# Two graph layers and two mixtures of experts on one core: a count matrix sent out in two pieces, the edge stage ahead of routing's constants, and four buffers for attention's first block

## The chip, the cores and the metric

The kernel runs on one core of one Trainium2 chip. A core has TensorE (matrix products into PSUM), VectorE, ScalarE, GpSimd (POOL here) and SyncE (SP, which only issues transfers). Each engine works through its own list of instructions in order and waits on semaphores for the others; SP, ScalarE (ACT) and POOL each issue DMA transfers on a queue of their own, and 16 DMA engines carry them. The metric is the device time of one execution in microseconds. A kernel is run several times, and the median counts.

## The reference, cut to what matters

`x` is 3125 nodes of 256 features, `src` and `dst` are 50,000 edges, `dst` sorted. Four layers, each added to `x` after a layer norm:

```python
edge_index = jnp.stack([src, dst])
x = x + gnn0(layernorm(x), src, dst)       # three graph convolutions, 256 -> 256, degree norms
x = x + ffn0(layernorm(x))                 # 16 experts, top 2 of them, then a layer norm with gamma, beta
x = x + gnn1(layernorm(x), edge_index)     # attention over the edges: 4 heads of 64
x = x + ffn1(layernorm(x))                 # 8 experts, top 2 of the softmax
# gnn0, one convolution:
h = h * norm_src[:, None] @ W
agg = segment_sum(h[src], dst)
out = agg * norm_dst[:, None] + b
# gnn1:
xa = h @ W;  el = xa @ Wl.T;  er = xa @ Wr.T
e = exp(leaky_relu(el[src] + er[dst], 0.2))
w = e / segment_sum(e, src)[src]
heads = [segment_sum(w[:, k:k+1] * xa[dst], src) for k in range(4)]
out = elu(stack(heads) + b)
```

## The kernel before, in words

The nodes are padded to NT = 25 tiles of 128 rows, of which REAL = 125 are nodes and three are padding. The seven destination blocks (BLK) hold 512 nodes four times (four tiles each) and then 384 three times (three tiles each). Both graph layers work with dense matrices of edge counts (how many edges lead from node a to node b), one per block, in fp16. They are built once, kept in DRAM in two layouts (`cnt`, source by destination, and `cntT`, its transpose) and loaded again, in groups of five source tiles, by every graph convolution and by attention.

A planner (Tile) lays out the order of each engine's instructions before the kernel runs. It goes through the program with durations that it assumes; whatever is ready on an engine may be taken, and among ready instructions the one that stands earlier in the program goes first. So a place in the program is a rank, not a time. It also gives out the memory: a tile that takes over another's room waits for the last reader of that room, transfers included.

The stages that matter here, in order:

**Constants.** Lines 707 to 743 make ramps, masks and token numbers for routing; `Router.__init__` (from line 745) makes further ones for each of the two mixtures and loads their gate weights over SP. In the program all of it stands ahead of the edges.

**Edge stage** (lines 1193 to 1311). `src` comes over SP and `dst` over ACT, three transfers each (L1214 to L1218). VectorE turns them into float (`nf`, L1221), then into tile numbers (`til`, L1225, L1226) and pairs (`edge`, L1227, L1228), which are written to DRAM in four shifted copies (`eds`, L1241, two on SP, two on ACT). POOL fills X's last rows with zeros (L1244) and SP loads X (L1246). VectorE finds where in the sorted list each of SG x 128 places begins by 16 comparisons summed up (L1279, L1285), for the first 128 places and then for the other four groups; POOL gathers the edges of each group from `eds` (L1302), and TensorE turns them (L1310) into `by`.

**Counting** (lines 1334 to 1385). For each run of nodes VectorE writes two one-hot matrices (`os`, L1349; `od`, L1352), TensorE multiplies them into counts (`pc`, L1354), ScalarE copies those into `cr` (L1357), which holds a block for all 25 source tiles and has two buffers. POOL clears the padding of `cr` first (L1340). After each destination tile TensorE transposes its columns (L1363), they go to `ct` (two buffers), and seven transfers on SP write them to `cntT` (L1372). After the last tile of a block one transfer on SP writes the whole of `cr` to `cnt` (L1378). At the ninth tile the layer norm's moments of X are taken.

**Graph convolutions** (lines 1407 to 1478). `cnt` is loaded (`cload`, L1421), cast by ScalarE (`ar`, L1452); the features, in two parts (`hi`, L1443, and the rest, L1446, on VectorE; `parts`, L1445, on ScalarE), are multiplied by it on TensorE (L1457). Layer 0 normalises X first (L1440, VectorE).

**End of the first mixture** (lines 1523 to 1594). Per block: two results of experts are added up (`rsum`, L1176), layer norms, `h` (L1554, ScalarE), transposes, the product with W (`px`, L1561, copied to `xT`, L1562), and a small product `py` (L1566), of which ScalarE copies out `xn` (L1567) and the factors `lr` (L1568). `tops` (L1569, VectorE) takes their largest. `xn` lies in the tile `spare`.

**Attention** (lines 1600 to 1746). ScalarE makes `xp`, the four heads' scaled copies of `xn`, tile by tile (L1718). For block b and source tile t VectorE writes the weights of all edges, `e`, four operations (L1730), into one of five buffers (three in HB, one of their own, and last `spare`), and TensorE multiplies them by `xp` (`att`) and sums them (`sums`), both L1618, in a fixed order. The buffer's number is

```python
ring.append(spare)
e = ring[(b * NT + t) % len(ring)]
```

In block b + 1 `finish` completes block b bit by bit, with VectorE and ScalarE work between the tiles. The second mixture follows.

Of the kernel before, what the change touches and what calls it, by code (L numbers as in the profile page):

```python
# [19 lines left out]
P = 128  # L20
# [574 lines left out]
def fast(  # L595
# [56 lines left out]
    consts = ctx.enter_context(tc.tile_pool(name="consts", bufs=1))  # L652
# [5 lines left out]
    cnt = [dram.tile([P, NT, w], F16, name=f"cnt{s0}") for s0, w in BLK]  # L658
    cntT = [dram.tile([P, NT, w], F16, name=f"cntT{s0}") for s0, w in BLK]

    ident = consts.tile([P, P], F32, name="ident")
# [42 lines left out]
                                    op0=OP.subtract, op1=OP.mult)  # L704


    iota_i = consts.tile([P, P], I32, name="iota_i")
    nc.gpsimd.iota(iota_i, pattern=[[1, P]], base=0, channel_multiplier=0)
    iota_r = consts.tile([P, P], F32, name="iota_r")
    nc.vector.tensor_copy(iota_r, iota_i)  # L710
    part_i = consts.tile([P, 1], I32, name="part_i")
    nc.gpsimd.iota(part_i, pattern=[[1, 1]], base=0, channel_multiplier=1)
    part = consts.tile([P, 1], F32, name="part")
    nc.vector.tensor_copy(part, part_i)
    before = consts.tile([P, P], BF16, name="before")
    nc.vector.tensor_scalar(before, iota_r, part, None, op0=OP.is_gt)
    ones = consts.tile([P, P], BF16, name="ones")
    nc.vector.memset(ones, 1.0)
    ones_f = consts.tile([P, P], F32, name="ones_f")
    nc.vector.memset(ones_f, 1.0)  # L720
    part_b = consts.tile([P, P], F32, name="part_b")
    nc.vector.tensor_copy(part_b, part.to_broadcast([P, P]))
    real = consts.tile([P, 1], F32, name="real")
    nc.vector.tensor_scalar(real, part, float(REAL), None, op0=OP.is_lt)
    unreal = consts.tile([P, 1], F32, name="unreal")
    nc.vector.tensor_scalar(unreal, part, float(REAL), None, op0=OP.is_ge)
    PADS = P - REAL
    drop = consts.tile([P, NT], F32, name="drop")
    nc.vector.tensor_scalar(drop, iota_r[:, :NT], float(2 * PADS), None, op0=OP.mult)
    nc.vector.scalar_tensor_tensor(drop, part.to_broadcast([P, NT]), float(-REAL), drop, op0=OP.add, op1=OP.add)  # L730
    assert 2 * NT * PADS <= 2 * P
    tok2 = consts.tile([P, NT], F32, name="tok2")
    nc.vector.tensor_scalar(tok2, iota_r[:, :NT], 2.0 * P, None, op0=OP.mult)
    nc.vector.scalar_tensor_tensor(tok2, part.to_broadcast([P, NT]), 2.0, tok2, op0=OP.mult, op1=OP.add)
    tok_i = consts.tile([P, NT], I32, name="tok_i")
    nc.gpsimd.iota(tok_i, pattern=[[P, NT]], base=0, channel_multiplier=1)


    metas = consts.tile([P, NT, 8], F32, name="metas")
    nc.vector.memset(metas, 0.0)  # L740
    nc.vector.tensor_copy(metas[:, :, 0], tok2)
    nc.vector.tensor_copy(metas.bitcast(I32)[:, :, 5], tok_i)
    places = consts.tile([P, 2, NT], I32, name="places")

    class Router:

# [431 lines left out]


    MAGIC = 12582912.0  # L1180
    ident16 = consts.tile([P, P], F16, name="ident16")
    nc.vector.tensor_copy(ident16, ident)
    ones16 = consts.tile([P, 32], F16, name="ones16")
    nc.vector.memset(ones16, 1.0)
    full = consts.tile([1, 1], F32, name="full")

    state = ctx.enter_context(tc.tile_pool(name="state", bufs=1))
    X = state.tile([P, NT, D], F32, name="X")
    HB = state.tile([P, NT * D], F32, name="HB")
    HBn = HB.rearrange("p (t d) -> p t d", d=D)  # L1190

    R0 = Router("m0", f0_gate_w, f0_gate_b, f0_gate_w.shape[1], False, consts)
    R1 = Router("m1", f1_gate_w, f1_gate_b, f1_gate_w.shape[1], True, consts)
    plans = ctx.enter_context(tc.tile_pool(name="plans", bufs=1))

    with tc.tile_pool(name="edges", bufs=1) as ed, tc.tile_pool(name="ework", bufs=2) as ew:
        by = [ed.tile([P, SG * P], dt, name=f"by{i}") for i, dt in enumerate((F16, F32))]
        with tc.tile_pool(name="epre", bufs=1) as ep, tc.tile_pool(name="ps_pre0", bufs=1, space=PSUM) as ps0, \
# [36 lines left out]
            for k in range(P // ST):  # L1235
# [8 lines left out]
            nc.gpsimd.memset(X[96:], 0.0)  # L1244
            for a, b in ((0, SPLIT), (SPLIT, REAL)):
                nc.sync.dma_start(X[a:b], x.rearrange("(t p) d -> p t d", p=REAL)[a:b])  # L1246


            base = ep.tile([P, SG * P], F32, name="base")
# [22 lines left out]
            for g0, g1 in ((0, 1), (1, SG)):  # L1272
                a, b = g0 * P, g1 * P
                n = 0
                for h in range(CH):
                    for o in range(0, P, ST):
                        one = nf[:, 1, h, o:o + 1]
                        if n == 0:
                            i = nc.vector.tensor_scalar(acc[:, a:b], base[:CR, a:b], one, None, op0=OP.is_gt)  # L1279
# [19 lines left out]
                at_e = ep.tile([P, SG], I32, name=f"at_e{g0}")  # L1299
                sent = nc.vector.tensor_tensor(at_e[:, G], f[:, G, 0], f[:, G, 1], op=OP.add)  # L1300
                for g in range(g0, g1):
                    nc.gpsimd.indirect_dma_start(  # L1302
                        out=got[:, g].rearrange("p e v -> p (e v)"), out_offset=None, in_=rows_e,
                        in_offset=bass.IndirectOffsetOnAxis(ap=at_e[:, g:g + 1], axis=0))
            for g in range(SG):

                nc.scalar.activation(key[:, g, :], got[:, g, :, 1], AF.Identity, bias=f[:, g, 3:4])
                for i, v in enumerate((got[:, g, :, 0], key[:, g, :])):
                    pt = ps_by.tile([P, P], F32, name="pt")
                    nc.tensor.transpose(pt, v, ident)  # L1310
                    nc.scalar.copy(by[i][:, g * P:(g + 1) * P], pt)

        ramp_i = ed.tile([P, 512], I32, name="ramp_i")
        nc.gpsimd.iota(ramp_i, pattern=[[1, 512]], base=0, channel_multiplier=0)
        ramp = ed.tile([P, 512], F16, name="ramp")
# [15 lines left out]
        with tc.tile_pool(name="ps_cnt0", bufs=2, space=PSUM) as ps_cnt0, \  # L1331
# [6 lines left out]
            for b, (s0, bw) in enumerate(BLK):  # L1338
                cr = ew.tile([P, NT, bw], F16, name="cr", tag="cr")
                nc.gpsimd.memset(cr.rearrange("p t (u q) -> p t u q", q=P)[:, :, :, REAL:], 0.0)  # L1340
                for dt in range(s0 // P, (s0 + bw) // P):
                    o = dt * P - s0
# [26 lines left out]
                    for b2, (q0, w2) in enumerate(BLK):  # L1369
                        nc.tensor.matmul(op[b2 // 4][32 * (b2 % 4):32 * (b2 % 4) + 32, :w2], ones16,  # L1370
                                         ct[:, q0:q0 + w2], start=(dt == 0), stop=(dt == NT - 1))
                        nc.sync.dma_start(cntT[b2][:, dt, :], ct[:, q0:q0 + w2])  # L1372
                    if dt == 1:
                        R0.clear(HB[:, 9 * R1.Q:])
                        R1.clear(HB[:, :9 * R1.Q])
                    if dt == 8:
                        mv, r = moments(X)
                nc.sync.dma_start(cnt[b], cr)  # L1378
# [128 lines left out]
    with tc.tile_pool(name="moe0", bufs=1) as mp:  # L1507
# [16 lines left out]
        with tc.tile_pool(name="ps_pre", bufs=2, space=PSUM) as ps, tc.tile_pool(name="tail", bufs=1) as mp:  # L1524
# [12 lines left out]
            for s0, w in BLK:  # L1537
# [26 lines left out]
                py = ps.tile([P, 4, OD + 2 * NH], F32, name="py", tag="py")  # L1564
                for i in range(n):
                    nc.tensor.matmul(py[:, i, :], xT[:, (t0 + i) * P:(t0 + i + 1) * P], turn, start=True, stop=True)  # L1566
                nc.scalar.copy(xn[:, t0:t0 + n, :], py[:, :n, :OD])  # L1567
                nc.scalar.copy(lr.rearrange("p t s h -> p t (s h)")[:, t0:t0 + n, :], py[:, :n, OD:])  # L1568
# [31 lines left out]
    with tc.tile_pool(name="gat", bufs=2) as gp, tc.tile_pool(name="aloads", bufs=2) as loads:  # L1600
        xp = gp.tile([P, NT, NH, OD], F32, name="xp", bufs=1)
        with tc.tile_pool(name="ps_att", bufs=2, space=PSUM) as ps_att, \
# [116 lines left out]
            for b, (s0, w) in enumerate(BLK):  # L1719
# [4 lines left out]
                for kg in range(0, NT, KG):  # L1724
                    a = load_cnt(loads, cntT[b], kg, w)
                    for k in range(KG):
                        t = kg + k
                        e = ring[(b * NT + t) % len(ring)]
                        for h in range(NH):
                            nc.vector.scalar_tensor_tensor(e[:, h, :w], ub[:, h, :w], wj[:, t, h:h + 1],  # L1730
                                                           a[:, k, :w], op0=OP.max, op1=OP.mult)
# [70 lines left out]
```

## Time and profile before

| | us |
|---|---|
| median of 3 runs (2017.44 to 2019.27) | 2019.27 |
| the profiled execution | 2025.07 |
| its span, first to last instruction | 2023.2 |
| TensorE busy | 1850.2 |
| VectorE busy | 1197.2 |
| ScalarE busy | 781.7 |
| edge stage and constants, until the first count | 52.3 |
| counting, until TensorE's last product | 297.2 |
| first graph convolution's first product | 304.9 |
| attention's first product | 1185.2 |
| mean granted TensorE clock, share of full | 0.955 |

Busy is the time in which an engine has an instruction under way; matrix products are pipelined, so a busy TensorE need not be at its peak. The span is also shown in 40 slices of 50.6 us, in each of which a digit gives the busy share in tenths. The timeline lists instructions by start, with like ones merged; in square brackets stands how long the engine was idle before and what ended that. `SPq`, `ACTq` and `POOLq` are the sequencers that issue transfers. The time of an issue is the time until the queue has taken it, not until it has landed. The trace also keeps a record of each packet of a transfer, with its size and time.

### The profile page before, as it was taken

To read this page: it belongs to the slowest core of one execution; us is meant where nothing else is said; L and a number is where in the kernel's file an instruction comes from. 1 tells how busy PE (TensorE), PEld (TensorE's weight loads), DVE (VectorE), ACT (ScalarE), POOL (GpSimd) and SP (SyncE) were. 2 spreads that over 40 slices of the span, in tenths; PEclk is the share of its full clock that TensorE was granted. 3 is DMA by queue.
4 is the path that set the end of the run, shared out by engine and by line. 5 is a ranking of instruction groups with operands and counts; after the bars stand their busy time and mean duration, and the time that the engine had idled before them with its cause. 6 is when DMAs were issued, how large, how long until landed. Compare 5 with 4: busy or idle time off the path is not lost. (4 is left out here: it accounts for less than half of the span.)

```text
span 2023.2 us, 31498 instructions
## 1 busy us (share of the span) xinstructions
PE 1850.2 (91%) x10742; PEld 1220.2 (60%) x10742; DVE 1197.2 (59%) x3811; ACT 781.7 (39%) x1571; POOL 368.8 (18%) x414
## 2 busy tenths in 40 slices
PE   1898979999999999699999979999999998699995
PEld 1444547898899889588898622223223233589893
DVE  7998864113103545544433958988998998444323
ACT  0367776556556555222232660212212222233230
POOL 5000000000000133354551000000300402444430
PEclk9999999999999999699998969999999999599996
DMA  6145664344434444765664401111111111456646
GB/s 165 39 179 213 229 231 132 112 123 134 130 108 143 126 113 125 228 196 189 205 208 145 161 13 53 44 46 51 41 44 50 39 40 29 119 190 201 202 144 198
DMA packets 172296, 259.87 MB, mean 128 GB/s; under 512 B 33476, under 2 KB 116658, under 8 KB 171100
## 3 DMA queue, kind: packets, MB, share of 16 engines
q1 hardware_dynamic: 148446, 211.87, 34.1%
q0 software_dynamic: 16016, 37.00, 5.5%
q10 hardware_dynamic: 7662, 8.84, 1.4%
q8 instruction: 91, 1.49, 0.3%
q14 instruction: 81, 0.66, 0.1%
HBM read 187.38 MB, written 70.27 MB: 127 GB/s over the span
## 5 line engine op out<-in xcount | busy, mean ns | idle before, releaser
L1457 PE MATMUL agg<-ar,parts 128*128 128x512 f32 (+1 forms) x2100 | 446.6, 371 | 7.6 <-ACT parts L1445 7.6
L1457 PEld LDWEIGHTS agg<-ar,parts 128*128 128x128 f32 x2100 | 382.3, 189 | 54.9 <-ACT parts L1445 7.7
L1730 DVE SCALAR_TENSOR_TENSOR HB<-ub,wj,cload 128x512 f32<-128x512 f32 (+1 forms) x420 | 268.5, 687 | 21.7 <-ACT ub L1634 9.9
L1452 ACT CAST ar<-cload 128x2560 fp32r<-128x2560 f16 (+1 forms) x105 | 220.8, 2103 | 145.8 <-PE agg L1457 131.2
L1049 ACT ACTIVATE hid<-ph,b1s 128x128 f32<-128x128 f32 x448 | 128.1, 369 | 315.3 <-PE ph L1045 315.3
L1045 PEld LDWEIGHTS ph<-xsT,w1t 128*128 128x128 f32 x1792 | 222.5, 197 | 25.9 <-DVE xsT L1035 14.6
L1045 PE MATMUL ph<-xsT,w1t 128*128 128x128 f32 x1792 | 231.3, 282 | 7.4 <-DVE xsT L1035 7.3
L1055 PE MATMUL py<-w2all,hid 128*128 x896 | 212.0, 380 | 0.0
L1618 PE MATMUL att<-HB,xp 128*64 128x512 f32 (+1 forms) x840 | 185.9, 563 | 0.0
L1460 DVE COPY aT<-agg 128x512 f32<-128x512 f32 (+1 forms) x21 | 13.3, 634 | 277.7 <-PE agg L1457 277.7
L1055 PEld LDWEIGHTS py<-w2all,hid 128*128 128x128 f32 x896 | 162.2, 191 | 17.5
L1352 DVE TENSOR_SCALAR od<-ramp,by 128x450 f16<-128x450 f16 (+11 forms) x588 | 151.5, 318 | 21.5 <-PE pc L1354 20.2
L1354 PE MATMUL pc<-od,os 128*128 128x450 f16 (+11 forms) x588 | 136.7, 334 | 17.9 <-DVE od L1352 10.4
L911 POOL DMA_INDIRECT slots_m<-metas,places x100 | 106.2, 1062 | 205.9 <-DVE places L909 110.1
L1072 POOL DMA_INDIRECT res_m<-y,to_i x112 | 110.7, 988 | 169.1 <-DVE y L1071 159.5
L1035 DVE COPY xsT<-misc 128x256 f32<-128x256 f32 x112 | 47.4, 424 | 138.2 <-PE misc L1033 138.2
L1024 POOL DMA_INDIRECT xs<-feats_m,slot x112 | 108.5, 969 | 89.7 <-PE misc L1033 64.4
L1618 PEld LDWEIGHTS att<-HB,xp 128*64 128x64 f32 x840 | 51.6, 136 | 106.7 <-issue 60.2
L1357 ACT CAST cr<-pc 128x400 f16<-128x400 f32 (+10 forms) x202 | 95.5, 503 | 51.0 <-PE pc L1354 49.4
L1354 PEld LDWEIGHTS <-os 128*128 128x128 f16 x588 | 62.2, 117 | 78.3 <-DVE od L1352 21.5
L1618 PE MATMUL sums<-HB,pj 128*32 128x512 f32 (+1 forms) x840 | 102.2, 558 | 0.0
L1071 DVE TENSOR_SCALAR y<-py,g 128x256 f32<-128x256 f32 x112 | 54.1, 483 | 70.6 <-PE py L1055 70.0
(338 smaller groups left out, 2259.7 us busy)
## 6 DMA issues: line engine op xcount, KB each, us to landing
cload<-cnt SPq DMA_DIRECT2D x60, 640.0 KB
w1t<-in_L_ffn_w_dram SPq DMA_DIRECT2D x56, 512.0 KB
w1t<-in_L_ffn_W_dram SPq DMA_DIRECT2D x52, 512.0 KB
cload<-cnt SPq DMA_DIRECT2D x45, 480.0 KB
cntT<-ct SPq DMA_DIRECT2D x100, 128.0 KB
cnt<-cr SPq DMA_DIRECT2D x4, 3200.0 KB
r<-res_m SPq DMA_DIRECT2D x50, 256.0 KB
cload<-cntT SPq DMA_DIRECT2D x20, 640.0 KB
```

What stands on the lines that cost most here:

```text
L911: d = nc.gpsimd.indirect_dma_start(out=self.slots, out_offset=bass.IndirectOffsetOnAxis(ap=at_i[:, u:u + 1], axis=0), in_=meta[:, u, :], i ...
L1024: nc.gpsimd.indirect_dma_start(out=xs, out_offset=None, in_=self.feats, in_offset=bass.IndirectOffsetOnAxis(ap=slot[:, 5:6].bitcast(I32), ...
L1045: behind(nc.tensor.matmul(ph[:, c, :], w1t[:, f, c * P:(c + 1) * P], xsT[:, f, :], start=(f == 0), stop=(f == DC - 1)), "PE")
L1049: nc.scalar.activation(hid[:, c, :], ph[:, c, :], func, bias=self.b1s[:, c, j:j + 1])
L1055: behind(nc.tensor.matmul(py, hid[:, c, :], w2all[:, bass.ds(r, 1), c, :].rearrange("p o d -> p (o d)"), start=(c == 0), stop=(c == FC - 1 ...
L1072: d = nc.gpsimd.indirect_dma_start(out=self.res, out_offset=bass.IndirectOffsetOnAxis(ap=to_i, axis=0), in_=y, in_offset=None)
L1352: nc.vector.tensor_scalar(od[:, :w * NT], ramp[:, :w * NT], by[1][:, j:j + 1], None, op0=OP.is_equal)
L1354: nc.tensor.matmul(pc[:, :w * NT], os_[:, :, j % OS], od[:, :w * NT], start=(k == 0), stop=(k == c - 1))
L1452: nc.scalar.copy(ar[:, :, :w], a[:, :, :w])
L1457: nc.tensor.matmul(agg[f][:, :w], parts[:, t, i, f * P:(f + 1) * P], ar[:, k, :w], start=(t == 0 and i == 0), stop=(t == NT - 1 and i == 1))
L1618: return chain(nc.tensor.matmul(*args, **kw))
L1730: nc.vector.scalar_tensor_tensor(e[:, h, :w], ub[:, h, :w], wj[:, t, h:h + 1], a[:, k, :w], op0=OP.max, op1=OP.mult)
```

## The change

Four things are changed.

1. The constants and both `Router` objects are made after the edge stage in the program, except `ones_f`. POOL no longer fills X's rows 96 to 127; VectorE makes a small tile of zeros (`none`, three rows) and a transfer on ACT writes it to X's three padding rows in all 25 tiles. X's load on SP stands behind the edge gathers and waits for the last of them.
2. The transfer of a block of counts becomes two: all columns but the last tile's, ranked right behind the last-but-one tile's `cntT` transfers, and the last tile's 128 columns at the end.
3. VectorE instead of ScalarE copies `lr` and `xn` out of PSUM, `lr` first.
4. In attention's block 0 the buffers are taken in turn from the first four alone.

The diff, cut to its core:

```diff
-    iota_i = consts.tile([P, P], I32, name="iota_i")
...
-    places = consts.tile([P, 2, NT], I32, name="places")
...
-    ident16 = consts.tile([P, P], F16, name="ident16")
...
-    R0 = Router("m0", f0_gate_w, f0_gate_b, f0_gate_w.shape[1], False, consts)
-    R1 = Router("m1", f1_gate_w, f1_gate_b, f1_gate_w.shape[1], True, consts)
...
-            nc.gpsimd.memset(X[96:], 0.0)
-            for a, b in ((0, SPLIT), (SPLIT, REAL)):
-                nc.sync.dma_start(X[a:b], x.rearrange("(t p) d -> p t d", p=REAL)[a:b])
...
-                    nc.gpsimd.indirect_dma_start(
+                    last_got = nc.gpsimd.indirect_dma_start(
                         out=got[:, g].rearrange("p e v -> p (e v)"), out_offset=None, in_=rows_e,
                         in_offset=bass.IndirectOffsetOnAxis(ap=at_e[:, g:g + 1], axis=0))
+            none = ep.tile([PADS, D], F32, name="none")
+            nc.vector.memset(none, 0.0)
+            nc.scalar.dma_start(X[REAL:], none[:, None, :].to_broadcast([PADS, NT, D]))
+            for a, b in ((0, SPLIT), (SPLIT, REAL)):
+                i = nc.sync.dma_start(X[a:b], x.rearrange("(t p) d -> p t d", p=REAL)[a:b])
+                tc.add_manual_dep(i.ins, last_got.ins.name, mybir.DependencyInfo(
+                    mybir.DependencyClass.Sync, mybir.DependencyReason.DATA), reason="the edges come first")
             for g in range(SG):
...
+        iota_i = consts.tile([P, P], I32, name="iota_i")
...
+        places = consts.tile([P, 2, NT], I32, name="places")
+
+        ident16 = consts.tile([P, P], F16, name="ident16")
...
+        R0 = Router("m0", f0_gate_w, f0_gate_b, f0_gate_w.shape[1], False, consts)
+        R1 = Router("m1", f1_gate_w, f1_gate_b, f1_gate_w.shape[1], True, consts)
         ramp_i = ed.tile([P, 512], I32, name="ramp_i")
...
+                    if o == bw - 2 * P:
+
+                        nc.sync.dma_start(cnt[b][:, :, :bw - P], cr[:, :, :bw - P])
...
-                nc.sync.dma_start(cnt[b], cr)
+                nc.sync.dma_start(cnt[b][:, :, bw - P:], cr[:, :, bw - P:])
...
-                nc.scalar.copy(xn[:, t0:t0 + n, :], py[:, :n, :OD])
-                nc.scalar.copy(lr.rearrange("p t s h -> p t (s h)")[:, t0:t0 + n, :], py[:, :n, OD:])
+                nc.vector.tensor_copy(lr.rearrange("p t s h -> p t (s h)")[:, t0:t0 + n, :], py[:, :n, OD:])
+                nc.vector.tensor_copy(xn[:, t0:t0 + n, :], py[:, :n, :OD])
...
-                        e = ring[(b * NT + t) % len(ring)]
+
+                        e = ring[t % (len(ring) - 1)] if b == 0 else ring[(b * NT + t) % len(ring)]
```

More of the change, by code (lines that the diff above doesn't have):

```diff
@@ L704, in normalise @@
                                     op0=OP.subtract, op1=OP.mult)
-    iota_i = consts.tile([P, P], I32, name="iota_i")
[L708 to L718, printed above, removed]
+    PADS = P - REAL
     ones_f = consts.tile([P, P], F32, name="ones_f")
     nc.vector.memset(ones_f, 1.0)
[L721 to L742, printed above, removed]
-    places = consts.tile([P, 2, NT], I32, name="places")
     class Router:
@@ L1180, in fast @@
     MAGIC = 12582912.0
-    ident16 = consts.tile([P, P], F16, name="ident16")
-    nc.vector.tensor_copy(ident16, ident)
-    ones16 = consts.tile([P, 32], F16, name="ones16")
-    nc.vector.memset(ones16, 1.0)
     full = consts.tile([1, 1], F32, name="full")
@@ L1311, in fast @@
                     nc.scalar.copy(by[i][:, g * P:(g + 1) * P], pt)
+        iota_i = consts.tile([P, P], I32, name="iota_i")
+        nc.gpsimd.iota(iota_i, pattern=[[1, P]], base=0, channel_multiplier=0)
+        iota_r = consts.tile([P, P], F32, name="iota_r")
+        nc.vector.tensor_copy(iota_r, iota_i)
+        part_i = consts.tile([P, 1], I32, name="part_i")
+        nc.gpsimd.iota(part_i, pattern=[[1, 1]], base=0, channel_multiplier=1)
+        part = consts.tile([P, 1], F32, name="part")
@@ new lines, in fast @@
+        nc.vector.tensor_copy(part, part_i)
+        before = consts.tile([P, P], BF16, name="before")
+        nc.vector.tensor_scalar(before, iota_r, part, None, op0=OP.is_gt)
+        ones = consts.tile([P, P], BF16, name="ones")
+        nc.vector.memset(ones, 1.0)
+        part_b = consts.tile([P, P], F32, name="part_b")
+        nc.vector.tensor_copy(part_b, part.to_broadcast([P, P]))
+        real = consts.tile([P, 1], F32, name="real")
+        nc.vector.tensor_scalar(real, part, float(REAL), None, op0=OP.is_lt)
@@ new lines, in fast @@
+        unreal = consts.tile([P, 1], F32, name="unreal")
+        nc.vector.tensor_scalar(unreal, part, float(REAL), None, op0=OP.is_ge)
+        drop = consts.tile([P, NT], F32, name="drop")
+        nc.vector.tensor_scalar(drop, iota_r[:, :NT], float(2 * PADS), None, op0=OP.mult)
+        nc.vector.scalar_tensor_tensor(drop, part.to_broadcast([P, NT]), float(-REAL), drop, op0=OP.add, op1=OP.add)
+        assert 2 * NT * PADS <= 2 * P
+        tok2 = consts.tile([P, NT], F32, name="tok2")
+        nc.vector.tensor_scalar(tok2, iota_r[:, :NT], 2.0 * P, None, op0=OP.mult)
@@ new lines, in fast @@
+        nc.vector.scalar_tensor_tensor(tok2, part.to_broadcast([P, NT]), 2.0, tok2, op0=OP.mult, op1=OP.add)
+        tok_i = consts.tile([P, NT], I32, name="tok_i")
+        nc.gpsimd.iota(tok_i, pattern=[[P, NT]], base=0, channel_multiplier=1)
+        metas = consts.tile([P, NT, 8], F32, name="metas")
+        nc.vector.memset(metas, 0.0)
+        nc.vector.tensor_copy(metas[:, :, 0], tok2)
+        nc.vector.tensor_copy(metas.bitcast(I32)[:, :, 5], tok_i)
+        places = consts.tile([P, 2, NT], I32, name="places")
@@ L1313, in fast @@
+        ident16 = consts.tile([P, P], F16, name="ident16")
+        nc.vector.tensor_copy(ident16, ident)
+        ones16 = consts.tile([P, 32], F16, name="ones16")
+        nc.vector.memset(ones16, 1.0)
+        R0 = Router("m0", f0_gate_w, f0_gate_b, f0_gate_w.shape[1], False, consts)
+        R1 = Router("m1", f1_gate_w, f1_gate_b, f1_gate_w.shape[1], True, consts)
         ramp_i = ed.tile([P, 512], I32, name="ramp_i")
```

## The prediction

> **What bounds the kernel now.** I read the page's busy shares and slices first, then the timeline (columns: start, time, engine, line, operation, tiles, count, idle before it and what ended it) at the places that the diff touches.
>
> ```profile
> PE 1850.2 (91%) x10742; PEld 1220.2 (60%) x10742; DVE 1197.2 (59%) x3811; ACT 781.7 (39%) x1571; POOL 368.8 (18%) x414
> ...
> PE   1898979999999999699999979999999998699995
> DVE  7998864113103545544433958988998998444323
> ```
>
> TensorE is the bound almost everywhere. The slices where it is low are what an edit can win: the first one (50.6 us wide), where VectorE has 7 tenths, and one before attention. The start, in the timeline:
>
> ```profile
> 2.75 0.47 SPq L1214 DMA_DIRECT2D idx<-in_src_dram  x1
> ...
> 6.23 0.69 DVE L1221 CAST nf<-idx 98x1024 f32<-98x1024 int32 x1 [4.21 <-DMA eds<-away]
> 6.32 5.97 POOL L1244 MEMSET X<- 32x6400 f32 x1
> ...
> 6.96 5.62 DVE L1225 TENSOR_SCALAR til<-nf 98x512 f32<-98x512 f32 x1
> ...
> 12.61 0.71 DVE L1226 TENSOR_SCALAR til<-til 98x512 f32<-98x512 f32 x1
> ...
> 13.96 1.20 DVE L710 CAST iota_r<-iota_i 128x128 f32<-128x128 int32 x1
> ...
> 19.30 0.69 DVE L1228 SCALAR_TENSOR_TENSOR edge<-nf,til 98x512 f32<-98x512 f32 x1
> ```
>
> L1225 takes 5.62 us and its twin L1226 0.71: it ends when POOL's fill of X ends. Then routing's constants (L710 to L772) stand ahead of L1228 for 5.25 us (14.05 to 19.30). VectorE's sums L1279/L1285 follow, and counting (PE L1354) starts at 52.28. The end of counting:
>
> ```profile
> 288.85 0.32 SPq L1378 DMA_DIRECT2D cnt<-cr  x1
> ...
> 298.59 5.58 DVE L1440 TENSOR_SCALAR HB<-X,mv,rn 128x256 f32<-128x256 f32 x17
> ...
> 300.25 2.33 ACT L1452 CAST ar<-cload 128x2560 fp32r<-128x2560 f16 x1 [3.16 <-DMA g0w<-in_L_gnn_W_dram]
> ...
> 304.86 13.15 PEld L1457 LDWEIGHTS agg<-ar,parts 128*128 128x128 f32 x47 [7.74 <-ACT parts L1445]
> ```
>
> TensorE idles 7.7 us: 17 normalisations stand ahead of the first `hi` on VectorE, and ScalarE's first `ar` waits for a transfer until 300.25. And attention's first block:
>
> ```profile
> 1193.34 0.75 DVE L1730 SCALAR_TENSOR_TENSOR spare<-ub,wj,cload 128x512 f32<-128x512 f32 x1
> 1194.01 6.71 DVE L1730 SCALAR_TENSOR_TENSOR HB<-ub,wj,cload 128x512 f32<-128x512 f32 x10
> ...
> 1197.87 1.07 PE L1618 MATMUL att<-spare,xp 128*64 128x512 f32 x2
> ...
> 1201.43 1.97 PE L1618 MATMUL att<-spare,xp 128*64 128x512 f32 x2 [2.49 <-DVE spare L1730]
> ...
> 1208.01 0.75 DVE L1730 SCALAR_TENSOR_TENSOR spare<-ub,wj,cload 128x512 f32<-128x512 f32 x1 [2.66 <-ACT xp L1718]
> ...
> 1212.65 1.94 PE L1618 MATMUL att<-HB,xp 128*64 128x512 f32 x8
> ```
>
> `spare` still holds `xn`, which ScalarE copies out until 1208; the fifth tile's factors go into it quarter by quarter, and TensorE waits for them.
>
> **Start.** (1) The source indices no longer queue behind four gate transfers of 0.47 us: SP can issue its three as ACT does its own now (0.75, 1.75, 2.21 instead of 2.75, 3.58, 4.36), so `nf` comes 2.1 us earlier. (2) The 5.97 us fill leaves POOL: L1225 falls to its twin's 0.71, 4.9 us less. The new fill of three rows (a memset near 0.15 us, one transfer of 75 rows on ACT) waits for nobody. (3) The constants leave the path before L1228 (5.25 us) but stay on VectorE: 24 operations of about 0.19 us, 4.6 us, behind the sums and ahead of or among the first counts, which VectorE sets (15.45 of 16 us busy from 84 to 100). At worst they cost 4.6; at best they fall into VectorE's waits for TensorE there (3.76 at 26.21, 0.68 at 33.37, 1.62 at 51.30). I take 3.6, so 1.6 gained. (4) VectorE operations stretched beside POOL's fills of HB (L785 2.06 against 0.34) may move: 0.9, between -1 and 2. The first gather (35.41 to 44.47, beside the X load) has no share in this: VectorE is in its sums until 48 anyway. Sum 9.5 us, ends 6 and 13. X now waits on SP for the last gather, near 45; behind it on SP stand the writes of `cntT`, the first at 84.05 (near 75 then). The load took 14.34 us to issue, so it is out by 60; X is first read at the ninth node tile. That wait costs nothing; were the gathers 15 us later, `cntT` would be late.
>
> **The block of counts in two pieces.** Now one transfer has 128 rows of 25600 or 19200 B, 949 or 714 ns each at the fast end of the trace's packet records: 8 rows on each of 16 engines, 7.6 or 5.7 us. Then each piece has 128 x 25 = 3200 rows, 200 an engine: the first of 768 B (36 ns in the records of `cntT` and `cload`) or 512 B (27 ns, `idx`), 7.2 or 5.4 us; the second of 256 B, for which the nearest row is the bias load, 18 ns, 3.6 us. How fast the queue makes such rows bounds it from the other side: the `cload` of 640 rows of 768 B starts one row in 2.1 ns at its best (6.7 us for 3200), in 3.4 over the whole (10.7 us), and the X load took 12.93 us to issue for 2800 rows, 4.6 ns each (14.7 us). Nearest in direction and number of rows there is none; I take 6.5 us for a first piece and 5 for a second, since the `cload` rate of 2.1 ns is that of a queue already running. Beside them a node tile's seven `cntT` transfers take about 3.4 us (111.51 to 114.86). A block of three tiles, 21.5 us long (245.92 to 267.40), then holds 10 + 11.5 = 21.7 us of one queue, which just fits, as `ct` has two buffers and so a tile of delay; a block of four, 30.3 us or more, holds 13.6 + 12. SP issues in order, so `cntT` stands behind the pieces. I take 1.5 us lost over three blocks (0 to 6). At the end the second piece is shorter than the whole (5 for 5.7 to 6.7) but queues behind the previous tile's late `cntT`: `ar` comes between 3 us earlier and 2 later. If the planner then lets `hi` go ahead of some of the 17, TensorE starts up to 4 us earlier. I take 1. Together -0.5 us, ends +4 and -8.
>
> The Trainium skill (DMA: Bandwidth & Descriptors, Specifications) says that transfers below 512 B fall short of the line rate because they are read, modified and written. No HWDGE write of 256 B rows is in this trace. By that rule the second piece would take about double, an estimate, and its result is that of the third rival below.
>
> **Copies to VectorE.** In blocks of four TensorE is busy 14.9 of 15 us (1140 to 1155), so nothing moves there: VectorE's wait for `lr` (1.06 us) is replaced by copies of about 0.37 and 0.19 us. In the last two blocks the chain runs over ScalarE:
>
> ```profile
> 1165.32 0.47 ACT L1562 COPY xT<-px 64x384 f32<-64x384 f32 x1 [1.47 <-PE px L1561]
> ...
> 1167.44 0.32 ACT L1567 COPY spare<-py 128x192 f32<-128x192 f32 x1 [1.64 <-PE py L1566]
> 1167.65 0.18 ACT L1568 COPY lr<-py 128x24 f32<-128x24 f32 x1
> 1167.72 1.10 ACT L1554 ACTIVATE h<-X,nm,rstd 128x256 f32<-128x256 f32 x2
> ```
>
> `h` needs `nm` of 1165.05 and stands behind copies that wait for `py`; without them it starts near 1165.8, 1.9 us earlier, and in the block before by 0.8 (1159.27 for 1158.4). After the last block `tops` waits for one engine fewer but for `xn` too: nothing. 2.5 us, ends -1 and 4.
>
> **Attention.** One node tile takes TensorE 2.86 us (1215.51 after 1212.65). The sixth was due at 1197.87 + 2.86 = 1200.73 and came at 1212.65: 11.9 us lost. With four buffers in block 0 the fifth goes into the first, free since 1192.2; VectorE needs 2.74 us a tile and has 8.6 to spare, ScalarE's `xp` 0.96 us a tile: the wait goes. It takes its price at the block's end: tile 24 uses buffer 0 and so does block 1's first (25 mod 5). That one starts when TensorE has let go: 0.75 us for a head, then three more of 0.67 before the last pair of products, so TensorE loses about 1.5 us. If VectorE's order puts tiles 1 to 4 of block 1 ahead, that is all. If it waits there, it loses its lead (9.2 us now); `finish` then adds 9.3 us of VectorE work by tile 13, of which 3.2 are not caught up. So 10.4 or 7.2 gained; the row at 1194.01, ten later operations ahead of the waiting tile, speaks for the first. I take 9.5.
>
> **Sum.** 9.5 - 0.5 + 2.5 + 9.5 = 21 us. The profiled execution took 2025.07 (2023.2 and 1.87 around the span), so 2004.1; it stands 5.8 us above the median 2019.27, so I predict 1998.3.
>
> **Rivals.**
> First, the rows choke SP's queue, and the kernel is slower. The place is counting's last three blocks: 10 us of `cntT` and two pieces of p fit 21.5 us up to p = 5.8 us; beyond it each microsecond of p costs 2 in every three-tile block, and from 8.4 in a four-tile one too. At p = 9 (2.8 ns a row) 3 x 6.4 + 1 us eat the 21 gained; at 12 (3.75 ns) 3 x 12.4 + 7 + 3 = 47 us, 2045. For it: X's 4.6 ns. Against it: the 2.1 ns, and X was read beside `eds` and `res` with the engines 99% busy. 0.13.
> Second, the small ends: constants wholly on the path, the lead lost in attention, no gain from the copies: 6 - 1.5 + 1 + 7.2 = 13, 2006. 0.2.
> Third, only the 256 B rows are slow, up to the X load's 4.6 ns each: the second piece takes twice 3.6 to 6.7 us, 7.2 to 13.4. The skill's rule would act like this. A three-tile block then holds 23 to 30 us, 1.5 to 8.5 too many, 5 to 25 us in all: 2003 to 2023, 2012 as its middle. 0.12.
> Fourth, the ends that help: 13 + 3 + 4 + 10.4 = 30, 1989. 0.1.
>
> **The numbers.** My forecast, 1992 to 2004, has 0.45. The range is 1987 to 2016: above it lie the first rival and the top of the third, below it part of the fourth. 0.2% (4 us) is about what these runs can tell from no change. Faster 0.82, within 0.2% 0.05 (third rival's top, and the first near p = 9), slower 0.13.
>
> **What would show it.** `nf` near 4, L1225 at 0.7 us, the edges written near 8 instead of 20, counting from 42 to 44. Two `cnt` transfers a block, with POOL's fill of `cr` earlier and ScalarE's waits of `ct` for `cntT` hardly above today's 5.8 us in sum: tens of microseconds there make the first or third rival true. TensorE's wait before L1457 between 4 and 9 us. No `spare` in block 0, no wait at tile 4, one of 1.5 to 2 at the turn to block 1; waits on L1730 in block 1 around tile 10 show the lost lead. The likeliest error is the queue's rate for 3200 short rows.

## The result, and the profile after

The changed kernel takes 2009.43 us (median of 6 runs, 2004.86 to 2012.87) where the kernel before takes 2019.92 (6 runs, 2017.44 to 2028.69): a ratio of 0.9933, 95% interval 0.9914 to 0.9952. By the ratio it is faster by 13.5 us (9.7 to 17.4), where I had forecast 21; the two medians lie 10.5 us apart. The profiled execution took 2009.38 us, span 2007.5, against 2025.07 and 2023.2 before.

To see where the time went, I note in both traces when TensorE begins the same product, and take the differences of the times between (after minus before):

| stretch, by TensorE's first product of each | before | after | difference | forecast |
|---|---|---|---|---|
| start: until the first count | 52.28 | 42.29 | -9.99 | -9.5 |
| counting, until the product `pn` at its end | 244.76 | 243.95 | -0.81 | together |
| border: until the first aggregation | 7.82 | 10.40 | +2.58 | +0.5 |
| three graph convolutions | 515.73 | 515.59 | -0.14 | 0 |
| first mixture, until its last part (`rsum`) | 279.56 | 280.03 | +0.47 | 0 |
| end of the first mixture, until attention's `pl` | 77.95 | 80.31 | +2.36 | -2.5 |
| attention | 532.98 | 523.38 | -9.60 | -9.5 |
| the rest | 312.16 | 311.58 | -0.58 | 0 |
| sum | 2023.24 | 2007.53 | -15.71 | -21 |

("attention" here runs from `pl` to its last `att` product.) The two big terms came within half a microsecond of their forecast. Two small ones have the wrong sign or size. TensorE's slices on the changed kernel's page:

```profile
PE   2898969999999999699999989999999998799995
```

TensorE's first slice went from 1 to 2 tenths: it is still the emptiest. The start, in the timeline:

```profile
5.00 0.69 DVE L1181 CAST nf<-idx 98x1024 f32<-98x1024 int32 x1 [2.71 <-DMA idx<-in_dst_dram]
5.73 0.44 DVE L1185 TENSOR_SCALAR til<-nf 98x512 f32<-98x512 f32 x1
6.20 0.43 DVE L1186 TENSOR_SCALAR til<-til 98x512 f32<-98x512 f32 x1
...
7.28 0.69 DVE L1188 SCALAR_TENSOR_TENSOR edge<-nf,til 98x512 f32<-98x512 f32 x1
...
26.43 1.13 POOL L1258 DMA_INDIRECT got<-eds,at_e  x1 [13.54 <-DVE at_e L1256]
26.57 4.69 DVE L1241 SCALAR_TENSOR_TENSOR acc<-base,nf,acc 98x512 f32<-98x512 f32 x6
27.56 4.20 POOL L747 MEMSET HB<- 128x3224 f32 x2
```

The edges are done at 7.97 instead of 19.99: `nf` 1.23 us earlier (it now waits for the destinations, which come over ACT), L1185 and L1186 5.46 us less, and the 5.25 us of constants gone from here. But the first gather is only 9.0 us earlier, not 12.0. The 3.0 us are lost ahead of the sums: from the end of the edges to the first operation of the sums (L1235, before L1279) it takes 5.39 us for 2.18. From there to the gather it takes 13.07 for 13.24, so the constants that now stand among the sums cost nothing. The operations that prepare the sums, L1208 to L1211, now stand beside POOL's fills of HB, beside which only constants stood before:

```profile
9.37 2.06 DVE L1209 CAST num<-num_i 128x640 f32<-128x640 int32 x1
9.64 1.37 POOL L744 MEMSET HB<- 25x1536 f32 x1
```

and the same operation in the kernel before:

```profile
20.43 0.49 DVE L1253 CAST num<-num_i 128x640 f32<-128x640 int32 x1
```

The end of counting, same view:

```profile
276.22 0.53 SPq L1379 DMA_DIRECT2D cnt<-cr  x1
279.23 6.69 SPq L1376 DMA_DIRECT2D cntT<-ct  x7
285.96 0.53 SPq L1385 DMA_DIRECT2D cnt<-cr  x1
287.79 8.16 DVE L1447 TENSOR_SCALAR HB<-X,mv,rn 128x256 f32<-128x256 f32 x25
291.92 2.33 ACT L1459 CAST ar<-cload 128x2560 fp32r<-128x2560 f16 x1 [5.64 <-DMA cnt<-cr]
295.86 0.50 DVE L1450 TENSOR_SCALAR hi<-HB 128x256 int32<-128x256 int32 x2
```

Two things are new. The last piece (L1385) leaves SP behind the seven `cntT` of the last tile; before, the whole block left ahead of them. And VectorE has all 25 normalisations ahead of the first `hi` instead of 17: 8.16 us for 5.58. (`ar`'s load had been issued at 115.86; what ends ScalarE's wait is the landing of the last piece.)

The last block but one at the end of the mixture:

```profile
1150.48 0.47 ACT L1569 COPY xT<-px 64x384 f32<-64x384 f32 x1 [2.44 <-PE px L1568]
...
1152.60 0.18 DVE L1574 COPY lr<-py 128x24 f32<-128x24 f32 x1 [1.33 <-PE py L1573]
...
1154.49 0.16 DVE L1557 SCALAR_TENSOR_TENSOR nm<-mv,rstd 128x3 f32<-128x3 f32 x1
...
1154.75 1.09 ACT L1561 ACTIVATE h<-X,nm,rstd 128x256 f32<-128x256 f32 x2 [0.66 <-DVE rs_q L683]
...
1155.40 1.18 PE L1564 MATMUL ptr<-ident,h 128*128 128x128 f32 x4 [2.84 <-ACT h L1561]
```

and the same block in the kernel before:

```profile
1157.43 0.47 ACT L1562 COPY xT<-px 64x384 f32<-64x384 f32 x1 [0.88 <-PE px L1561]
...
1159.27 1.08 ACT L1554 ACTIVATE h<-X,nm,rstd 128x256 f32<-128x256 f32 x2
...
1159.92 1.17 PE L1557 MATMUL ptr<-ident,h 128*128 128x128 f32 x4 [1.08 <-ACT h L1554]
```

`h` no longer waits behind the copies on ScalarE, but the copies now stand on VectorE ahead of the operations that make `nm`, and wait there for `py`: `h` starts 4.27 us after `xT` was begun, where before it was 1.84, and TensorE waits 2.84 us for it instead of 1.08. In the last block it is the other way round: `h` starts 0.38 us after `xT` was begun (1161.43 after 1161.06), before 2.40, and TensorE waits 0.53 us instead of 0.99. And attention, at the fifth tile of block 0 and at the turn to block 1:

```profile
1192.64 1.94 PE L1625 MATMUL att<-HB,xp 128*64 128x512 f32 x8
...
1195.50 1.94 PE L1625 MATMUL att<-HB,xp 128*64 128x512 f32 x8
...
1257.86 3.06 PE L1625 MATMUL att<-HB,xp 128*64 128x512 f32 x8 [0.82 <-DVE HB L1738]
```

Tiles follow each other in 2.86 us with no wait; at the turn TensorE waits 0.82 us and the products take 3.06 for 1.94, as their factors come one by one.

Last, the transfers of counts. What ended most of ScalarE's and VectorE's waits for `ct` in this kernel, from the view of that tile (columns: what ended the wait, us in all, times):

```profile
  PE pt L1367: 19.5, 23
  DMA cntT<-ct: 3.0, 4
```

The second line was 6.0 in 8 waits before; new is one wait of 0.8 us that a load of `cnt` ended. By the packet records a last piece (3200 rows of 256 B) starts its rows within 3.84 to 4.13 us (1.2 to 1.3 ns a row, a packet 15 to 16 ns), a first one of 512 B rows within 5.77 to 6.36. I had forecast 5 and 6.5 us.

### The profile page after: what moved, and what is told of

Read it like the earlier page. It is cut to its first block, busy times and chain, and to the rows that moved or that the text cites. A ratio compares the mean times of both kernels' runs of the same rounds, so it can differ in the third digit from the quotient of the medians.

```text
span 2007.5 us, 31545 instructions
## 1 busy us (share of the span) xinstructions
PE 1845.5 (92%) x10742; PEld 1220.1 (61%) x10742; DVE 1190.3 (59%) x3826; ACT 778.9 (39%) x1557; POOL 366.3 (18%) x413
## 5 line engine op out<-in xcount | busy, mean ns | idle before, releaser
L1464 PE MATMUL agg<-ar,parts 128*128 128x512 f32 (+1 forms) x2100 | 446.4, 371 | 10.2 <-ACT parts L1452 10.2
L1738 DVE SCALAR_TENSOR_TENSOR HB<-ub,wj,cload 128x512 f32<-128x512 f32 (+1 forms) x436 | 278.8, 692 | 18.7 <-ACT ub L1641 8.9
L1625 PE MATMUL att<-HB,xp 128*64 128x512 f32 (+1 forms) x872 | 195.1, 565 | 0.8 <-DVE HB L1738 0.8
L1021 PEld LDWEIGHTS py<-w2all,hid 128*128 128x128 f32 x896 | 161.9, 191 | 17.4
L1625 PE MATMUL sums<-HB,pj 128*32 128x512 f32 (+1 forms) x872 | 106.5, 560 | 0.0
```

What stands on the lines that cost most here:

```text
L1021: behind(nc.tensor.matmul(py, hid[:, c, :], w2all[:, bass.ds(r, 1), c, :].rearrange("p o d -> p (o d)"), start=(c == 0), stop=(c == FC - 1 ...
L1464: nc.tensor.matmul(agg[f][:, :w], parts[:, t, i, f * P:(f + 1) * P], ar[:, k, :w], start=(t == 0 and i == 0), stop=(t == NT - 1 and i == 1))
L1625: return chain(nc.tensor.matmul(*args, **kw))
```

## The experiments

Stage times are taken from the traces as above. The total of a single execution says less: TensorE's granted clock differs between executions in places that no edit touches, by some 2 to 4 us in a stage (the first mixture's products `ph`, first to last, took 224.99 and 226.15 us at a mean clock of 0.99 in two of the first six kernels, 227.95 to 229.37 at 0.98 in the other four).

### The start alone

`e1_start` is the changed kernel with parts 2, 3 and 4 undone.

> The new start alone; counting's pieces, the copies and attention's buffers as before. Theory (the parts do not depend on each other): the first count at 42.3 us as in the changed kernel (before: 52.28), so 10.0 us gained there; TensorE's wait ahead of the first aggregation back at 7 to 8 us (changed: 10.2); the products px to the first pl back at 55.8 us (changed: 58.4); the stall in attention's first block stays at 11.9 us. The span ends about 10 us below that of before. Rival (an earlier start is given back at the border, because what counting waits for there does not move): the wait before the first aggregation is 10 us in this kernel too, and only 7 to 8 us are kept.

Measured: first count at 42.06, the border 7.82 us as before, from the first `px` to the first `pl` 55.92; the stall in attention is there (block 0 90.3 us, before 88.9). Span 2013.0, 10.2 below before. The start's gain is kept whole through the border, and the rival falls: what was lost there belongs to another part.

### The four buffers alone

```diff
-                        e = ring[(b * NT + t) % len(ring)]
+                        e = ring[t % (len(ring) - 1)] if b == 0 else ring[(b * NT + t) % len(ring)]
```

> The kernel before with only the four buffers in attention's first block. Theory: block 0 of attention 10.7 us shorter, the turn to block 1 about 1.1 us longer, everything else within 0.3 us a stage: 9.6 us gained. Rival (VectorE, with no stall in which to run ahead, loses its lead, and later blocks wait): over 1 us lost in blocks 1 to 6 beyond the turn.

Measured: block 0 77.77 us for 88.89 (-11.1), block 1 80.43 for 79.31 (+1.1), blocks 2 to 6 within 0.1 us. VectorE's lead is not lost, and the rival falls.

### The copies back on ScalarE

```diff
-                nc.vector.tensor_copy(lr.rearrange("p t s h -> p t (s h)")[:, t0:t0 + n, :], py[:, :n, OD:])
-                nc.vector.tensor_copy(xn[:, t0:t0 + n, :], py[:, :n, :OD])
+                nc.scalar.copy(xn[:, t0:t0 + n, :], py[:, :n, :OD])
+                nc.scalar.copy(lr.rearrange("p t s h -> p t (s h)")[:, t0:t0 + n, :], py[:, :n, OD:])
```

> The changed kernel with the copies of py back on ScalarE. Theory (the copies stand in VectorE's order ahead of rstd and nm and wait there for py, so the next block's h comes late): from the first px to the first pl 55.8 us again, as before, not 58.4. Rival (the stretch depends on when the expert rows of the first layer's tail arrive, and it shifted by the start's 10 us): it stays at 58 us or more with the copies on either engine.

```profile
1146.96 0.47 ACT L1569 COPY xT<-px 64x384 f32<-64x384 f32 x1 [0.88 <-PE px L1568]
...
1147.74 0.16 DVE L1557 SCALAR_TENSOR_TENSOR nm<-mv,rstd 128x3 f32<-128x3 f32 x1
1148.40 0.32 ACT L1574 COPY spare<-py 128x192 f32<-128x192 f32 x1 [0.97 <-PE py L1573]
...
1148.80 1.08 ACT L1561 ACTIVATE h<-X,nm,rstd 128x256 f32<-128x256 f32 x2
...
1149.45 0.93 PE L1564 MATMUL ptr<-ident,h 128*128 128x128 f32 x4 [1.08 <-ACT h L1561]
```

The stretch from `px` to `pl` takes 55.10 us, as short as before. `nm` is ready before the copies on ScalarE, which then hold `h` up by 1 us; on VectorE they hold it up by more. The whole difference to the changed kernel is not the copies', though: the granted clock of the last three blocks was 0.53, 0.50 and 0.75 there and 1.00, 0.53 and 0.75 here. So I compare how long TensorE is idle. The last line of the windows (the sum over the stretch from the first `rsum` to the first `pl`; the idle time is the stretch less PE), of before, of the changed kernel, of this one:

```profile
sum 77.95, PE 69.57 PEld 45.55 DVE 54.61 ACT 40.54 POOL 0.00; mean PE 8.70 PEld 5.69 DVE 6.83 ACT 5.07 POOL 0.00
```

```profile
sum 80.31, PE 70.35 PEld 46.42 DVE 56.91 ACT 37.82 POOL 0.00; mean PE 8.79 PEld 5.80 DVE 7.11 ACT 4.73 POOL 0.00
```

```profile
sum 76.05, PE 67.42 PEld 44.53 DVE 54.40 ACT 40.50 POOL 0.00; mean PE 8.43 PEld 5.57 DVE 6.80 ACT 5.06 POOL 0.00
```

8.4, 10.0 and 8.6 us idle: the copies on VectorE cost 1.3 to 1.6 us of waiting. The other runs repeat it: from the first `px` to the first `pl` TensorE is idle for 8.0 to 8.3 us in eight kernels that copy on ScalarE, before the next block's `h`, and for 9.6 to 9.9 in the three with the copies on VectorE as in the changed kernel. The rest of the 2.4, as far as these runs tell, is the clock. Whether the longer wait itself lowers the clock they do not show: with the same wait of 2.84 us the clock of that block was 0.53 in the changed kernel and 0.74 in `e4_whole`.

### Counts written whole

```diff
-                    if o == bw - 2 * P:
-                        nc.sync.dma_start(cnt[b][:, :, :bw - P], cr[:, :, :bw - P])
...
-                nc.sync.dma_start(cnt[b][:, :, bw - P:], cr[:, :, bw - P:])
+                nc.sync.dma_start(cnt[b], cr)
```

> The changed kernel with each block of counts written whole, as before. Order theory (the last piece was issued on SP behind the last tile's seven transposed writes, as the planner ranks it by the work behind it): the whole write stands ahead of those seven again, VectorE has 17 normalisations ahead of hi instead of 25, and TensorE waits 7.6 us before the first aggregation instead of 10.2. Rows theory (short rows of 256 B land late): the same 7.6 us here; the kernel with the second piece placed ahead of those seven tells the two apart. Rival (the border's loss comes from the start: 10 us earlier, the weights for ar or VectorE's arrears are where they were): 10 us with the whole write too. Counting's blocks, from the first count to its end, within 0.5 us of either kernel.

```profile
277.77 0.32 SPq L1382 DMA_DIRECT2D cnt<-cr  x1
279.19 7.32 SPq L1376 DMA_DIRECT2D cntT<-ct  x7
287.90 5.58 DVE L1444 TENSOR_SCALAR HB<-X,mv,rn 128x256 f32<-128x256 f32 x17
293.40 0.48 DVE L1447 TENSOR_SCALAR hi<-HB 128x256 int32<-128x256 int32 x2
```

7.63 us of waiting for 10.21, 17 normalisations for 25; counting 244.33 us for 243.95. The pieces lose 2.6 us at the border, and in all runs the border takes 10.40 or 10.41 us with pieces and 7.82 or 7.83 without. In counting no gain or loss is shown: it took 243.70 to 245.68 us in the four kernels with pieces and 243.45 to 244.97 in the others. The copies are on VectorE here too, with the same wait of 2.84 us for `h` and 10.2 us idle in all, but at a better clock the stretch from `px` to `pl` took 55.78 us: the 58.4 of the changed kernel were not the copies' alone.

### The second piece first

```diff
+                    if o == bw - P:
+                        nc.sync.dma_start(cnt[b][:, :, bw - P:], cr[:, :, bw - P:])
                     ct = ew.tile([P, NP], F16, name="ct")
...
-                nc.sync.dma_start(cnt[b][:, :, bw - P:], cr[:, :, bw - P:])
```

> The changed kernel with the second piece of each block ranked ahead of the last node tile's transposes, so that SP issues it before that tile's seven cntT. VectorE's list keeps 25 normalisations ahead of the first hi. Theory 1 (VectorE's 25 normalisations set TensorE's wait ahead of the first aggregation): the piece lands earlier, ScalarE's first ar starts before 291, and TensorE still waits 9.5 us or more. Theory 2 (the late piece sets it, by way of ar): the wait falls to 7.7 us or below.

```profile
279.23 3.75 SPq L1363 DMA_DIRECT2D cnt<-cr  x1
283.07 8.73 SPq L1378 DMA_DIRECT2D cntT<-ct  x7
289.40 8.16 DVE L1448 TENSOR_SCALAR HB<-X,mv,rn 128x256 f32<-128x256 f32 x25
293.36 2.33 ACT L1460 CAST ar<-cload 128x2560 fp32r<-128x2560 f16 x1 [5.46 <-DMA cntT<-ct]
297.47 0.49 DVE L1451 TENSOR_SCALAR hi<-HB 128x256 int32<-128x256 int32 x2
298.25 2.07 PE L1465 MATMUL agg<-ar,parts 128*128 128x512 f32 x4 [10.22 <-DMA g0b<-in_L_gnn_b_dram]
```

The piece's issue begins 6.7 us earlier (and takes 3.75 us for 0.53), and TensorE waits as long as ever, 10.22 us. (The row names `g0b`; the weight load of the same product names `parts`, which needs `hi`.) `ar` did not come before 291 as I had expected: its load was issued at 116.81, but ScalarE waited until the last tile's `cntT`, now behind the piece, had landed. It is done at 295.69 all the same, and `hi` starts at 297.47, right behind the 25th normalisation. So the 25 normalisations set the wait: 8.16 less 5.58 is the 2.58 us that the border lost. Why the planner puts 25 of them ahead stays open. A guess that I have not shown: `hi` takes over room of counting's buffers, and in the planner's reckoning that room comes free later when the transfers come in pieces.

### X's fill alone, the constants alone, both

`e5_fill` replaces POOL's fill of X by the transfer of zeros, in the kernel before; `e6_consts` moves the constants and both `Router` objects behind the edges and leaves the fill; `e9_fill_consts` does both, with X's load left where it was.

> The kernel before with one edit: the rows of X that hold no node are filled by a transfer of three rows of zeros, not by the 5.97 us fill on POOL. Theory (VectorE's L1225 is held up by POOL's fill): L1225 falls from 5.62 to 0.7 us, or to 1 to 2.5 where it meets the next fills on POOL (HB's, 1.4 us each, which move up); the first count 3 to 5 us earlier than 52.28, at 47.4 to 49. Rival (VectorE waits there for something else, the indices or its own 98 partitions): L1225 stays above 5 us and the first count at 52.

> The kernel before with routing's constants behind the edges alone (so the source indices are first on SP too); POOL's fill of X and X's load stay at their place. Theory by the prediction's terms: 2.1 us for the indices and 1.6 for the constants, so the first count near 48.6; with the fill of the last kernel's edit the two make the 10.0 of the whole. Rival (the 5.25 us of constants hide wholly behind the waits for sums): 2.1 + 5.25, the first count at 45. Other rival (POOL's fill, still 5.97 us, starts earlier and holds up the operations that now stand next to it): under 2 us gained.

> The kernel before with the two start edits of the last two runs together (the fill by a transfer, the constants behind the edges), and X's load where it was, not held behind the gathers. Theory (the two hold each other up: with either alone VectorE's copies and one-operand operations meet one of POOL's fills, with both they don't): the first count at 42 to 43.5, the whole gain of the start, and holding X's load back adds nothing. Rival (X's early load delays the edges' way through DRAM and the gathers): 45 or later.

Measured: the first count at 49.74, 53.72 and 43.13, against 52.28 before: 2.5 us gained, 1.4 us lost, 9.2 us gained. L1225 fell to 0.71 us with the fill gone, so that cause is shown, and yet half of the gain went again (the edges are written 5.2 us earlier, the first count comes 2.5 us earlier). From `e5_fill`, VectorE and POOL:

```profile
32.30 4.20 POOL L781 MEMSET HB<- 128x3224 f32 x2
35.15 3.96 DVE L785 TENSOR_SCALAR HB<-HB 128x403 f32<-128x403 int32 x1 [1.65 <-POOL HB L781]
...
38.17 0.54 POOL L787 MEMSET HB<- 128x203 f32 x1
```

and from `e6_consts`:

```profile
5.94 5.59 POOL L1205 MEMSET X<- 32x6400 f32 x1
6.20 5.62 DVE L1186 TENSOR_SCALAR til<-til 98x512 f32<-98x512 f32 x1
...
31.21 0.42 DVE L1317 CAST ramp<-ramp_i 128x512 f16<-128x512 int32 x1
...
32.21 7.11 DVE L1321 CAST ramps<-ramp_i 128x512 f16<-128x512 int32 x1
32.63 4.20 POOL L747 MEMSET HB<- 128x3224 f32 x2
...
38.50 0.54 POOL L753 MEMSET HB<- 128x203 f32 x1
```

In each, one operation of VectorE meets POOL's chain of fills of HB and ends 0.3 to 0.4 us after that chain: 3.96 us and 7.11 us, where its like takes 0.36 to 0.53 and 0.42. In the changed kernel the three-operand sums L1241 stand beside the same fills (26.57 to 31.26, six in 4.69 us, 0.78 each) and are not held up, but for one behind an `od` that is (32.51, 1.53 us for 0.75). So the gain of the start is not a sum of its parts: it depends on which operation stands beside which fill. Holding X's load back is worth 0.8 to 1.1 us (43.13 against 42.29 and 42.06, and 42.18 in `b1_start_ring`, which ran on the same chip as `e9_fill_consts`); the forecast had given it nothing, since the first gather was to have no share. In `e9_fill_consts` that gather is issued at 26.58, TensorE begins to turn the edges (`pt`) at 31.14, and VectorE idles 1.90 us for `by`; in the changed kernel the two are at 26.43 and 29.53.

### The copies on VectorE, behind the next block's `nm`

```diff
+                first = nc.vector.scalar_tensor_tensor(nm, mv[:, :, 0], -1.0, r, op0=OP.mult, op1=OP.mult)
+                if later:
+                    out_of(*later, first)
```

(`out_of` makes the copies of the block before and has them wait for `first`.)

> The changed kernel, its copies of py still on VectorE, but made to stand behind the next block's nm. Theory (the place in VectorE's order costs, not the engine): TensorE's wait for h in the last block but one falls from 2.84 us to below 1.1, its idle time from the tail's first rsum to the first pl from 9.96 us to 8 or less (copies on ScalarE: 8.6), and the stretch from the first px to the first pl is 54 to 56 us at a like clock. Rival (the copies are simply more work for an engine that has none to spare): idle time stays near 10.

```profile
1153.94 0.13 DVE L1568 SCALAR_TENSOR_TENSOR nm<-mv,rstd 128x3 f32<-128x3 f32 x1
...
1154.17 1.09 ACT L1574 ACTIVATE h<-X,nm,rstd 128x256 f32<-128x256 f32 x2 [0.35 <-DVE nm L1568]
...
1154.82 1.18 PE L1577 MATMUL ptr<-ident,h 128*128 128x128 f32 x4 [1.81 <-ACT h L1574]
```

The wait for `h` fell to 1.81, not to 1.1, and idle time to 9.6 us (77.60 less 68.04), not to 8: by that figure the rival is nearer. My theory of the order holds for 1.0 of the 1.8 us by which that wait had grown over ScalarE's; for the rest `nm` itself is late (2.34 us after `xT` was begun; 0.78 with the copies on ScalarE). That VectorE's own work, which grew from 54.6 to 56.6 us in this stretch, makes it so is as the rival has it, but not shown.

### A faster version

`b1_start_ring` keeps the start and the four buffers and undoes the other two parts. `b2_best` adds two edits:

```diff
+                    first = nc.scalar.activation(h, X[:, t0 + i, :], AF.Identity, bias=nm[:, i:i + 1], scale=r[:, i:i + 1])
+                    if later and i == 1:
+                        out_of(*later, first)
...
+            order = 4, 1, 2, 3, 0
...
-                        e = ring[t % (len(ring) - 1)] if b == 0 else ring[(b * NT + t) % len(ring)]
+                        e = ring[t % (len(ring) - 1)] if b == 0 else ring[order[((b - 1) * NT + t) % len(ring)]]
```

> The changed kernel with counts written whole and the copies of py back on ScalarE, so only the start and attention's four buffers remain. Theory: 10.5 us from the start, 9.6 from attention, nothing lost at the border (7.6 us of waiting) or in the tail: about 20 us below before, ratio 0.990, and some 4 us below the changed kernel. Rival (the losses seen in single profiles are the granted clock's, not the edits'): as the changed kernel, 0.993.

> As the last one, with two more edits: the copies of py on ScalarE are made to stand behind the second h of the next block, and from block 1 on the buffers are taken in the order 4, 1, 2, 3, 0, so that block 1 begins with the one that block 0 left free. Theory: the turn to block 1 gives back its 1.1 us; h, which waited for the copies in the two last blocks, starts 0.8 to 1.9 us earlier in each, so 2 to 4 us below the last kernel, ratio 0.988 to 0.989. Rival (later copies hold up hT on ScalarE, and the tops at the end come later): within 1 us of the last kernel.

These ran on another chip, on which the kernel before takes 2031.01 us (11 runs), so only the ratios compare: 0.9906 (0.9887 to 0.9924) for the first, 0.9885 (0.9864 to 0.9907) for the second, where the changed kernel has 0.9933 (0.9914 to 0.9952). `b2_best` beats both kernels; against `b1_start_ring` the intervals overlap, and the traces have to tell. Their totals cannot: the profiled span of `b2_best` is 1.4 us the longer (2010.1 and 2008.7), with 2.9 and 4.0 us lost in the first mixture and in the rest, which the two edits do not touch. Attention's blocks 0 and 1 took 168.20 us before, 158.59 in the changed kernel, 158.48 in `b1_start_ring` and 156.23 in `b2_best`: with the freed buffer first in block 1 TensorE has no wait for VectorE left in them, and the whole stall of 11.9 us is won, not 9.6. The end of the mixture had 7.7 us idle (78.00 less 70.34; before 8.4). The two edits together were expected to bring 2 to 4 us: the buffers brought 2.3, the copies some 0.9 of idle time (8.5 in `b1_start_ring`). `h` came 0.5 and 0.6 us earlier after `xT` in the last two blocks, not 0.8 to 1.9.

## Why the prediction was off, by its own steps

**The sum.** Of the 5.3 us between the 21 forecast and the 15.7 in the two traces, 4.9 are the end of the first mixture (the 2.5 that did not come, 1.6 of waiting, the rest most likely the clock) and 1.3 the counts; the start gave 0.5 more, attention 0.1, the untouched stretches 0.2. The forecast of 1998.3 was low by a further 5.8: I took the gain from the median of the three runs shown, while the traced execution of before stood 5.8 us above it and the traced one of the changed kernel at its median (2009.38 and 2009.43). Part of the 15.7 is thus the luck of one execution, and 13.5 us by the ratio, or 10.5 by the medians, are the better figures. The measured time lies within the range, 1987 to 2016.

**Start: right in sum, and nearly in its terms.** Indices 1.2 (2.1 forecast), the fill 5.5 (4.9), constants 2.2 (1.6), the rest 1.0 (0.9). The constants' 2.2 is 5.25 less 3.0, and that came about otherwise than I had it: most constants run among the sums for nothing, and the 3.0 go ahead of the sums, where operations are held up beside POOL's fills. I had added the terms as if each could be had alone. The runs with one of them move the first count by +1.4 and -2.5 us, since a fill of POOL then meets an operation that the sums wait behind; which operation meets which fill was in no step of mine but the fourth, with 0.9. (That step compared L785's 2.06 us with the 0.34 of a narrower one; its like takes 0.53 in the changed kernel.)

**Counts in two pieces: the queue was no danger, the planner was.** Rivals one and three are wrong: 3200 rows of 256 B took 4 us and not 5 or more, waits of `ct` for `cntT` fell. The Trainium skill (DMA: Bandwidth & Descriptors, Specifications) puts the smallest transfer for line rate at 512 B, because a smaller one is read, modified and written. The trace agrees in that rows of 256 B moved 198 to 213 GB/s and rows of 512 B 258 to 284. The doubling of the time was my own estimate and did not come. The step that failed is "If the planner then lets `hi` go ahead of some of the 17": it went the other way, to 25. I had named `ar` and `hi` as the two things TensorE waits for, and priced the transfer with care; the end that came last was VectorE's list, which I only hoped about. `ar` came 2.5 us later after `pn` than before (5.68 for 3.21) and was still done 1.6 us before `hi` began.

**Copies to VectorE: the wrong sign.** The step "without them it starts near 1165.8, 1.9 us earlier" came true in the last block: `h` starts 2.0 us earlier after `xT`. But I had put the whole of that down as gain, and TensorE's wait for it fell by 0.46 us, from 0.99. The step that failed is "in the block before by 0.8": it looked at the queue that the copies leave and not at the one that they join. On VectorE `rs_q`, `rstd` and `nm` of the next block stand behind them, and `h` needs `nm`; `h` came 2.4 us later and TensorE's wait grew by 1.8. Held behind `h` on ScalarE (`b2_best`), the copies free the start of `h` in both blocks, by 0.5 and 0.6 us.

**Attention: right.** The stall of 11.9 us went, and 2.3 of it came back, 2.0 at the turn (3.76 and 3.98 us from tile to tile for 2.86), where I had forecast 1.5. The lost lead that I had feared, 3.2 us not caught up, did not come.

**The rivals.** The median, 2009.43, lies between the second rival (small ends, 2006) and the middle of the third (slow short rows, 2012), and neither mechanism held: constants, lead and rows did well, copies and border did badly. (The fourth rival's sum takes 3 for the counts, whose end was 4.)

## What to carry to other kernels

When work moves from one engine to another, read what stands behind it in the list that it joins, and who waits for that; an engine with idle time can still be late at the one place that counts. Where a planner lays out the order, an edit of a transfer can reorder an engine that it doesn't touch: compare the lists, not only the transfers. And what a removed wait gives is bounded by the next thing late: the buffer order at the turn of two loops was worth 2.3 us beside the 11.9 of the stall. An earlier start of one operation is not a gain of that size either: the gain is at most the wait that it ends.

## What the runs showed of the hardware

VectorE's casts and one-tensor operations that stood beside a fill of POOL here stopped until it ended, in places for a whole chain of fills: 5.62 us instead of 0.44 to 0.71 beside the fill of X, 7.11 instead of 0.42 beside those of HB. Sums of two tensors (L1241) go on: 0.78 us beside the fill, 0.75 without. The Trainium skill (SBUF — State Buffer, SBUF: two separate sides) states such a lock: the two engines share a pair of ports, which one holds for a whole instruction, and which VectorE needs in its fast modes, while an operation with two inputs meets it only where POOL reads. The trace agrees on both kinds of operation, though it does not show the mode that an operation ran in; that VectorE waits through several fills in a row, 32.6 to 39.0 in `e6_consts`, is more than the one instruction that the Trainium skill speaks of.
